# Loading the first weight of a two-layer recurrence: which queues carry its four chunks, and which engine clears two small tiles

## The chip, the cores and the metric

The kernel runs on one core of a Trainium2 chip. A core has a matrix engine (TensorE, PE in the profile), three engines for elementwise work (VectorE or DVE, ScalarE or ACT, GpSimd or POOL) and a synchronisation engine (SyncE or SP). Loads and stores are done by 16 DMA engines that the core's queues share; a transfer is *issued* by an instruction on SyncE, ScalarE or GpSimd and *lands* some microseconds later, when its completion semaphore is counted up. The metric is the device time of one execution in microseconds. The kernel before takes 1639.33 us, the median of three runs from 1638.49 to 1639.35.

## What is computed

The input x has 128 sequences of 128 steps with 512 features, all in fp32. Two recurrent layers follow one another, each added to its input:

```python
# layer 0, for each step t; Wh, Wz are the two halves of W
gate = sigmoid(h @ Wh.T + z_t @ Wz.T + b)
h    = tanh(h * (1 - alpha) + gate * z_t)      # z = x, h starts as cond
x    = x + hs
# layer 1, for each step t
h    = tanh(x_t @ Wx + b + h @ Wh)             # h starts as cond
x    = x + hs
```

The products of the input with Wz and with Wx don't depend on the state and can be done for several steps at once; the products of the state with the two Wh are done step by step.

## The kernel before, in words

The features lie on the 128 partitions in 4 blocks, the sequences on the free axis, so that one step of x is a tile of 128 x 512. Tiles arrive in the natural order and VectorE transposes them in blocks of 32 x 32 (lines 198 to 216). Steps go in groups of four. Layer 1 follows layer 0 by nine steps. The input products of a group are done with a fast scheme of seven products in place of eight, for most groups nested in itself; those of the first steps are done plainly (`input_product`, line 467, its matmuls at L475), and the first nested group (steps 4 to 7) plainly with one level (L357). `state_product` (L464) does a step's state products.

The order of work is written by hand: `at(time, fn, ...)` enters a call into a plan, the plan is sorted by the time given, and every call then records its instructions in that order, so each engine's own instruction order follows from the plan. The times are only sorting keys; what runs when is settled by semaphores.

Around the change, at the start, the plan does the following:

- `clear_small` (line 166) writes zeros to `condT` (128 x 512, later the transposed start state) and to `rows` (32 x 96, into which three small vectors are loaded later, L172). `warm_up` (line 181) does five matmuls on the zeros of `condT`, into banks that are not read.
- `load_x` (line 125) loads a step of x in four quarters of 32 partitions, 64 KB each, going round the queues that it is given (L128). `both` is SyncE and ScalarE.
- `load_w0(1, "wz", chunks, engines)` (line 138) loads Wz in four chunks m = 0 to 3; a chunk is again four quarters of 64 KB, going round the queues given (L147). Without queues it goes to SyncE and ScalarE in turn.
- As the chunks come, `transpose_w0` (L212, VectorE) turns one chunk after the other, and `input_product` multiplies step 0 with it on TensorE; then step 1, then the plain products of group 1 (L357), for which steps 4 to 7 are transposed by VectorE and added up (L238) by VectorE and GpSimd.
- `load_w0(0, "wh0")` loads the state weight of layer 0, `load_cond` the start state; the state products begin after the plain products of group 1.

Transfers don't each have a semaphore of their own. The transfers of SyncE and ScalarE together go round eight completion semaphores (lanes), four for each as they alternate here, and those of GpSimd round another eight. An issue that comes back to a lane first waits until the lane's previous transfer has landed. So SyncE's fifth issue waits for its first to land, and GpSimd's ninth for its first.

Within the first 13 us the issues before are, in order: SyncE and ScalarE each x0 (2), chunk 0 (2), chunk 2 (2), chunk 3 (2), x5 (2), x7 (2), then the state weight (2) and cond (2); GpSimd chunk 1 (4), x1 (4), x4 (4), x6 (4), small rows (3). The x7 issues also wait until the tile of x0 is free again (five x tiles are there).

The functions that the change touches, with the line numbers of the profile:

Of the kernel before, what the change touches and what calls it, by code (L numbers as in the profile page):

```python
# [13 lines left out]
def kernel(  # L14
# [35 lines left out]
    nc = tc.nc  # L50
# [23 lines left out]
    def at(time, fn, *args):  # L74
        plan.append((time, len(plan), fn, args))
# [47 lines left out]
    both = (nc.sync, nc.scalar)  # L123
# [35 lines left out]
    rows = const.tile([S, 3, S], F32, tag="rows", name="rows")  # L159
# [4 lines left out]
    condT = const.tile([P, C, P], F32, tag="condT", name="condT")  # L164

    def clear_small():
        nc.gpsimd.memset(condT, 0.0)
        nc.gpsimd.memset(rows, 0.0)

    def load_small():  # L170
        for i, v in enumerate((b0, alpha, b1)):
# [377 lines left out]


    at(0.0, clear_small)
    at(0.01, warm_up)
    at(0.1, load_x, 0, both)
    at(0.2, load_w0, 1, "wz", (0,))
    at(0.21, load_w0, 1, "wz", (1,), (nc.gpsimd,))
    at(0.22, load_w0, 1, "wz", (2, 3))
    at(0.3, load_x, 1, (nc.gpsimd,))
    at(0.31, load_x, 4, (nc.gpsimd,))
    at(0.4, load_x, 5, both)
    at(0.41, load_x, 6, (nc.gpsimd,))  # L560
# [166 lines left out]
```

## Time and profile before

| what | before |
|---|---|
| median of 3 runs | 1639.33 us |
| the profiled execution's own time | 1639.27 us |
| its span, first to last instruction | 1637.4 us |
| first GpSimd issue (chunk 1) | 1.40 us |
| x0 transposed from | 4.70 us |
| chunks 0, 1, 2, 3 transposed from | 6.64, 7.65, 8.75, 10.81 us |
| first product with Wz from | 7.41 us |
| product with chunk 3 from | 11.58 us |
| first state product from | 26.51 us |

The page gives the busy time of each engine and its share of the span. A chain of waits is followed back from the last instruction: at each step to what released it. The timeline lists instructions by start, duration, engine, line, operation and tiles, with the idle time before and what ended it in brackets; a "q" behind the engine's name marks its instruction queue, which issues transfers. L147 is line 147 of the kernel. Times inside the execution count from the span's start.

### The profile page before, as it was taken

What the parts mean: (1) busy time and instruction counts of PE and PEld (TensorE: products, weight loads), DVE (VectorE), ACT (ScalarE), POOL (GpSimd) and SP (SyncE); (2) the same over time, 40 slices, a digit from 0 to 9 for tenths busy, and PEclk for the clock granted to TensorE, in tenths of its full rate; (3) what the DMA queues carried; (4) which work ended last, traced back from release to release, by engine and by line L of the source; (5) the groups of instructions that cost most, each with busy time, mean ns of one, the idle gap of its engine ahead of it and who ended that gap; (6) DMA issues with size and microseconds to landing.
All of it is one profiled execution on the core that took longest, in us unless ns stands there. A gap on an engine that the chain in (4) does not pass through costs nothing.

```text
span 1637.4 us, 36984 instructions
## 1 busy us (share of the span) xinstructions
PE 1628.1 (99%) x14420; PEld 1621.8 (99%) x14420; DVE 1315.5 (80%) x2958; ACT 791.4 (48%) x2047; POOL 666.6 (41%) x548
## 2 busy tenths in 40 slices
PE   9999999999999999999999999999999999999998
PEld 8999999999999999999999999999999999999998
DVE  6677888878888888888787888888878888878785
ACT  2545445544454444444554545445545454454454
POOL 5553433344334333443344334433443344334442
PEclk9999999999999999999999999999999999999999
DMA  8201221121112111221112111211111112111113
GB/s 176 53 18 40 46 46 40 40 47 46 40 40 48 45 40 40 46 47 40 40 45 48 40 40 44 49 40 40 45 43 45 39 42 51 40 40 29 26 21 65
DMA packets 152078, 73.99 MB, mean 45 GB/s; under 512 B 16992, under 2 KB 150624, under 8 KB 151904
## 3 DMA queue, kind: packets, MB, share of 16 engines
q1 hardware_dynamic: 147936, 69.01, 18.7%
q10 hardware_dynamic: 3360, 1.57, 0.5%
q8 instruction: 113, 1.85, 0.5%
q0 software_dynamic: 608, 1.06, 0.3%
q14 instruction: 61, 0.50, 0.1%
HBM read 38.02 MB, written 33.55 MB: 44 GB/s over the span
## 4 chain that ended last, share of the span: by engine, by line
PE 96%; DVE 1%; ACT 1%; issue 1%; DMA 1%; POOL 0%; ACTq 0%; SPq 0%; DVEq 0%; POOLq 0%
PE r0a L464 14%; PE r0b L464 14%; PE r1b L464 14%; PE r1a L464 13%; PE B_b L363 12%; PE A_a L363 11%; PE A_b L363 9%; PE B_a L363 8%; DMA wz_in<-in_L_cond_W_dram 1%; PE A_a L357 0%; PE r1a L475 0%; DVE h L512 0%; PE B_a L357 0%; PE r0a L475 0%; PE B_b L357 0%
## 5 line engine op out<-in xcount | busy, mean ns | idle before, releaser
L520 POOL TENSOR_TENSOR T<-T,h 128x512 f32<-128x512 f32 x255 | 325.4, 1276 | 947.5 <-ACT h L517 880.8
L464 PE MATMUL r0a<-h,wha 128*128 128x128 f32 x2032 | 248.0, 275 | 0.2
L464 PE MATMUL r0b<-h,whb 128*128 128x128 f32 x2032 | 247.9, 275 | 0.0
L464 PE MATMUL r1a<-h,wha 128*128 128x128 f32 x2032 | 247.6, 275 | 0.0
L464 PE MATMUL r1b<-h,whb 128*128 128x128 f32 x2024 | 246.8, 275 | 0.0
L517 ACT ACTIVATE h<-h 128x256 f32<-128x256 f32 x256 | 106.7, 417 | 280.2 <-DVE h L512 278.7
L464 PEld LDWEIGHTS r0a<-h,wha 128*128 128x128 f32 x2032 | 237.4, 192 | 0.9 <-DVE r0a L452 0.5
L464 PEld LDWEIGHTS r0b<-h,whb 128*128 128x128 f32 x2032 | 237.1, 192 | 0.1
L464 PEld LDWEIGHTS r1a<-h,wha 128*128 128x128 f32 x2032 | 237.1, 192 | 0.0
L464 PEld LDWEIGHTS r1b<-h,whb 128*128 128x128 f32 x2024 | 236.2, 192 | 0.0
L503 ACT ACTIVATE r0a<-r0a,per_feature 128x128 f32<-128x128 f32 x256 | 87.6, 342 | 104.2 <-PE r0a L464 100.1
L509 DVE TENSOR_TENSOR r0a<-r0a,T 128x256 f32<-128x256 f32 x128 | 55.0, 429 | 84.1 <-ACT r0a L503 84.1
L509 DVE TENSOR_TENSOR r1a<-r1a,T 128x256 f32<-128x256 f32 x128 | 55.3, 432 | 67.7 <-ACT r1a L503 67.7
L205 DVE STREAM_TRANSPOSE o<-T 128x512 f32<-128x512 f32 x127 | 89.5, 705 | 4.1 <-POOL T L520 3.6
L200 DVE STREAM_TRANSPOSE T<-x 128x512 f32<-128x512 f32 x128 | 86.9, 682 | 6.0 <-DMA x<-in_x_dram 5.0
L503 ACT ACTIVATE r1a<-r1a,per_feature 128x128 f32<-128x128 f32 x256 | 85.2, 333 | 4.2
L530 ACT ACTIVATE h<-r1b,per_feature 128x128 f32<-128x128 f32 x255 | 80.4, 370 | 7.7 <-PE r1b L464 5.4
L530 ACT ACTIVATE h<-r0b,per_feature 128x128 f32<-128x128 f32 x256 | 78.0, 355 | 11.1 <-PE r0b L464 9.3
L238 POOL TENSOR_TENSOR S_b<-T 128x512 f32<-128x512 f32 x64 | 82.0, 1281 | 0.2
L512 DVE SCALAR_TENSOR_TENSOR h<-h,leak,r0a 128x128 f32<-128x128 f32 x254 | 77.0, 345 | 5.2
L512 DVE SCALAR_TENSOR_TENSOR h<-h,leak,r1a 128x128 f32<-128x128 f32 x254 | 77.0, 345 | 4.5
L391 ACT COPY ca<-A_a 128x896 f32<-128x896 f32 (+1 forms) x31 | 27.7, 895 | 101.7 <-PE A_a L363 101.7
(221 smaller groups left out, 3723.9 us busy)
## 6 DMA issues: line engine op xcount, KB each, us to landing
out_dram<-o SPq DMA_DIRECT2D x510, 64.0 KB, 1.8
x<-in_x_dram SPq DMA_DIRECT2D x494, 64.0 KB, 2.3
wx_in<-in_L_cond_Wx_dram SPq DMA_DIRECT2D x4, 256.0 KB, 5.4
wh_in<-in_L_cond_Wh_dram SPq DMA_DIRECT2D x4, 256.0 KB, 8.7
x<-in_x_dram POOLq DMA_DIRECT2D x12, 64.0 KB, 4.2
wh_in<-in_L_cond_W_dram SPq DMA_DIRECT2D x2, 256.0 KB, 6.3
wh_in<-in_L_cond_W_dram ACTq DMA_DIRECT2D x2, 256.0 KB, 6.8
x<-in_x_dram ACTq DMA_DIRECT2D x6, 64.0 KB, 4.2
```

The costliest lines, as they stand in the source:

```text
L200: nc.vector.transpose(dst.rearrange("p c (a i) -> p c a i", i=S), src.rearrange("p a (c j) -> p c a j", j=S))
L205: nc.vector.transpose(dst.rearrange("p a (c j) -> p c a j", j=S), src.rearrange("p c (a i) -> p c a i", i=S))
L238: eng.tensor_tensor(out(which), one(), two(), op)
L363: nc.tensor.matmul(sets[tag][:, n], self.right(outer, i), self.left(g, outer, i), start=first and n % 4 == 0, stop=True, skip_group_check= ...
L391: nc.scalar.copy(self.part(g, 1, 0)[:, n], sets[tag][:, n])
L464: nc.tensor.matmul(banks[m * (len(banks) - 1)][0][:, m], self.wh[:, c, 2 * half + m, :], h[t - 1][:, c], start=alone and n == 0, stop=c == ...
L503: nc.scalar.activation(gate[:, m], gate[:, m], AF.Sigmoid, bias=per_feature[:, 0, f : f + 1])
L509: nc.vector.tensor_tensor(gate, gate, at_of(t)[:, two[i]], ALU.mult)
L512: nc.vector.scalar_tensor_tensor(h0[t][:, f], h0[t - 1][:, f], leak[:, f : f + 1], gate[:, m], ALU.mult, ALU.add)
L517: nc.scalar.activation(h0[t][:, two[i]], h0[t][:, two[i]], AF.Tanh)
L520: (eng or nc.gpsimd).tensor_tensor(at_of(t)[:, part], at_of(t)[:, part], h[t][:, part], ALU.add)
L530: nc.scalar.activation(h1[t][:, f], ps[:, m], AF.Tanh, bias=per_feature[:, 2, f : f + 1])
```

## The change

The two clears are recorded on VectorE in place of GpSimd. Chunk 0's four quarters go to GpSimd, GpSimd, SyncE and ScalarE. Chunk 1 goes to SyncE and ScalarE, chunks 2 and 3 to GpSimd. The load of x1 goes from GpSimd to SyncE and ScalarE, behind the chunks in the plan as before. Nothing else changes in what is loaded or computed.

```diff
     def clear_small():
-        nc.gpsimd.memset(condT, 0.0)
-        nc.gpsimd.memset(rows, 0.0)
+        nc.vector.memset(condT, 0.0)
+        nc.vector.memset(rows, 0.0)
...
     at(0.0, clear_small)
     at(0.01, warm_up)
     at(0.1, load_x, 0, both)
-    at(0.2, load_w0, 1, "wz", (0,))
-    at(0.21, load_w0, 1, "wz", (1,), (nc.gpsimd,))
-    at(0.22, load_w0, 1, "wz", (2, 3))
-    at(0.3, load_x, 1, (nc.gpsimd,))
+    at(0.2, load_w0, 1, "wz", (0,), (nc.gpsimd, nc.gpsimd, nc.sync, nc.scalar))
+    at(0.21, load_w0, 1, "wz", (1,))
+    at(0.22, load_w0, 1, "wz", (2,), (nc.gpsimd,))
+    at(0.23, load_w0, 1, "wz", (3,), (nc.gpsimd,))
+    at(0.3, load_x, 1, both)
     at(0.31, load_x, 4, (nc.gpsimd,))
     at(0.4, load_x, 5, both)
     at(0.41, load_x, 6, (nc.gpsimd,))
```

The issues are then, in order: SyncE and ScalarE each x0 (2), chunk 0 (1), chunk 1 (2), x1 (2), x5 (2), x7 (2), state weight (2), cond (2); GpSimd chunk 0 (2), chunk 2 (4), chunk 3 (4), x4 (4), x6 (4), small rows (3). On VectorE the two clears stand ahead of the transpose of x0.

## The prediction

> **What bounds the kernel now.** I read the page first, then the waits of TensorE, then the chain of the first 14 us, then the timeline and single transfers there. The page's span and busy lines:
>
> ```profile
> span 1637.4 us, 36984 instructions
> PE 1628.1 (99%) x14420; PEld 1621.8 (99%) x14420; DVE 1315.5 (80%) x2958; ACT 791.4 (48%) x2047; POOL 666.6 (41%) x548
> ```
>
> TensorE is busy for all but 9.3 us of the span, and the table by stage has it at 500.00 of 500.00 us between 500 and 1000. So what this change can give lies in the few idle microseconds of the start, and it reaches the end one for one. The waits of TensorE, us in total, times, longest:
>
> ```profile
> PE r0a L475 <- DVE wa L212: 1.4, 1, 1.4
> PE r0b_-1_99 L185 <- POOL condT L167: 1.3, 1, 1.3
> PE r1a L475 <- DVE wa L212: 0.9, 1, 0.9
> PE B_b L363 <- DVE cb L387: 0.6, 1, 0.6
> ```
>
> Two waits on the transposed first weight (1.4 and 0.9 us) are all that the change aims at; the 1.3 us is the start of the warm-up. The chain of waits of the first 14 us (start, duration, what):
>
> ```profile
> 2.19 4.26 DMA wz_in<-in_L_cond_W_dram
> ...
> 6.47 4.15 DMA wz_in<-in_L_cond_W_dram
> ...
> 10.81 0.72 DVE wa L212
> ...
> 11.58 1.16 PE r1a L475 x8
> 12.74 1.34 PE r0a L475 x12
> ```
>
> Two transfers stand one behind the other: ScalarE's fourth issue (chunk 0, at 2.19) lands at 6.45, and only then may ScalarE issue its eighth (the last quarter of chunk 3, at 6.47), because each queue reuses a completion lane after four issues. It lands at 10.62, VectorE transposes from 10.81, TensorE starts on it at 11.58 and then has no gap: 27.40 us busy of the 27.40 from 11.60 to 39.00. The moment 11.58 is what the change must move. From the timeline, GpSimd and VectorE:
>
> ```profile
> 0.75 0.52 POOL L167 MEMSET condT<- 128x512 f32 x1 [0.29 <-POOLq L713]
> 1.21 0.17 POOL L168 MEMSET rows<- 32x96 f32 x1
> 1.40 2.35 POOL L147 DMA_DIRECT2D wz_in<-in_L_cond_W_dram  x4
> ...
> 6.64 0.71 DVE L212 STREAM_TRANSPOSE wa<-wz_in 128x512 f32<-128x512 f32 x1 [1.23 <-DMA wz_in<-in_L_cond_W_dram]
> ...
> 7.65 0.71 DVE L212 STREAM_TRANSPOSE wa<-wz_in 128x512 f32<-128x512 f32 x1 [0.29 <-DMA wz_in<-in_L_cond_W_dram]
> ```
>
> GpSimd loses 0.65 us to clearing before its first issue, and VectorE's transposes of chunks 0 and 1 each wait for a landing. Last, the stage table (PE, PEld, DVE, ACT, POOL busy, clock, DMA share, GB/s), and then GpSimd's issues of x (ns min/median/max):
>
> ```profile
> 7.40:10.70 3.30, 3.27 (x24) 2.90 (x24) 1.42 (x2) 0.00 (x0) 3.12 (x7) 1.00 1.14 236
> ```
>
> ```profile
> L128 POOL DMA_DIRECT2D x<-in_x_dram x12: 548/548/551, 3.7 to 10.0; - x12
> ```
>
> The DMA engines are full (share 1.14) at 236 GB/s, so 64 KB takes 0.28 us of them. One GpSimd issue takes 0.55 us (the first of all 0.71).
>
> **The change part by part.** *The two clears* go from GpSimd to VectorE, which does nothing until 4.70. No row shows VectorE clearing; GpSimd's clear took 0.52 us, and VectorE's passes over 128x512 take 0.65 to 0.71. So condT is ready at 1.27 to 1.46 and the warm-up starts between 0.06 us earlier and 0.13 later than its 1.33. I take zero: x0 hides it (lands at 4.50), and the warm-up ends before the first product. GpSimd's first issue moves from 1.40 to 0.75.
>
> *Chunk 0.* GpSimd issues its first two quarters at 0.75 and 1.46, SyncE and ScalarE one each as their third issues (1.66 and 1.70). GpSimd's second transfer of before landed 4.2 us after its issue: 1.46 + 4.2 = 5.66. ScalarE's third landed at 5.39; with one more transfer ahead, 5.67. So chunk 0 is complete near 5.7 instead of 6.45, its transpose starts at 5.9 (0.19 later, as before) and TensorE at 6.66 (0.77 after the transpose's start, as before) instead of 7.41.
>
> *Chunk 1* leaves GpSimd for SyncE and ScalarE, as their fourth and fifth issues. The fifth waits for the queue's first x0 transfer. ScalarE's fifth of before was issued at 3.30 and landed 4.5 us later, at 7.82. GpSimd now has five transfers issued by 3.3 instead of four, 0.28 each, and x0 itself may be late by as much: 7.8 to 8.4. Transpose at 8.0 to 8.6, product at 8.8 to 9.35. TensorE did three chunks from 7.41 to 10.68, 1.09 each, so chunk 2 is done at 11.0 to 11.5. Chunk 1 gets later by 0.2 to 0.8 us against 7.52, GpSimd's landing of before.
>
> *Chunks 2 and 3* go to GpSimd as its issues 3 to 10. Issue 6 is at 3.66, so chunk 2 lands by 3.66 + 4.2 = 7.9, before 8.56 of now. Issue 10 is at 0.75 + 0.71 + 8 x 0.55 = 5.86. Its lane is that of GpSimd's second issue (eight lanes there), landed at 5.66, so there is no wait. GpSimd's issues at 5.36 and 5.90 landed 4.3 and 4.1 later: chunk 3 is in at 9.95 to 10.15 instead of 10.62, and could be multiplied from 10.9 to 11.1.
>
> *The later loads.* SyncE and ScalarE each issue one transfer fewer before x5, x7, the state weight and cond, all of which come one slot sooner. x1 goes to them as sixth and seventh issues, gated by landings at about 4.2 to 5.7, so in by 9.9; VectorE transposes it only after chunk 3, near 11.0 instead of 11.45. On GpSimd x4, x6 and the three small rows stand two issues later, less 0.65: 1.10 - 0.65 = 0.45 us. x4 lands near 12.3 (before: 11.94), and VectorE, which took it at 12.61, takes it near 12.4. x6 lands near 14.9 (14.45); VectorE took it at 14.57, then x7 at 15.56 after a wait of 0.28 for its landing. x7 now comes first, so both are done by 16.4 instead of 16.27. The sums over them follow at 16.31 and end at 17.72; TensorE first wants them at 19.39, so the slack is 1.67 us, less what the start gains. The rows, now gated by VectorE's clear too, land near 17.4 (16.87) and are read at 23.83. The state weight lands sooner than 20.63; first read at 20.82 and needed at 26.30. All of this costs nothing while those margins stand; x6 landing 1.2 us later than reckoned would start to cost.
>
> *The sum.* Chunk 3 is multiplied from the later of 10.9 to 11.1 (its own landing) and 11.0 to 11.5 (end of chunk 2). I take 11.1, as chunk 1's landing has its nearest row at the early end (the fifth ScalarE issue, whose gate is unchanged). 11.58 - 11.1 = 0.5 us earlier, and nothing behind has a gap. Ends for the unknowns: -0.7 and +2.1 (below). The profiled execution of before took 1639.27, 1.87 outside its span; 0.5 less is 1638.8. The median shown is 1639.33, 0.06 above; from there it is also 1638.8.
>
> **Two rules of the Trainium skill against this.** The rows first: transfers landed nearly in the order of issue whichever queue issued them (4.50 for x0's last, 10.62 for chunk 3's last), with the engines full. "DMA: Bandwidth & Descriptors", section "Issuing engines are not separate DMA queues", says that starting transfers from several engines saves only the issuing time. By it alone the gain is the one transfer that GpSimd starts earlier, 0.28 us, and the time 1639.0; my sum adds what the lane waits give. The second: GpSimd's issues took 548 to 551 ns though VectorE's transposes at 4.70, 6.64 and 8.75 ran beside them. "SBUF — State Buffer", section "SBUF: two separate sides", says that certain VectorE operations lock GpSimd out of writing descriptors; were the clears such, GpSimd would start at 1.40 as before, chunk 3 would come at 10.65 and the time would be 1639.3. No trace here shows a VectorE clear.
>
> **The rivals.** *A, hidden by chunk 1:* the fifth issues on SyncE and ScalarE land late (8.4 or later), TensorE does chunks 1 to 3 back to back from 9.4, chunk 3 starts at 11.5. For it: full engines, two GpSimd transfers ahead. Against: the gate, x0's landing, hardly moves. Time 1639.3.
>
> *B, slower, GpSimd's queue as the bound:* ten weight transfers now go through one queue that keeps only its share of full engines. SyncE's and ScalarE's shares let four transfers through each from chunk 0's end (6.45) to chunk 3's (10.62), 1.04 us apiece. Ten at that pace from the first packet (2.3: the trace has its first packets 1.6 us after the issue at 1.40, now at 0.75) end at 12.7, 2.1 us later than 10.62: 1641.4. Against: until 12 us GpSimd's queue moved 0.95 of 2.38 MB, 40% and not a third; at that rate its ten would take 6.3 us. It decides once a GpSimd transfer takes over 0.83 us, (10.62 - 2.3) / 10.
>
> *C, the clock:* the warm-up's ten passes are 0.43 us apart, the same shape in L357 is 1.73 / 8 = 0.22 apart, and L475 runs fast from 7.41, so the clock rose between. With warm-up or first product moved, the rise may come after chunk 0; each chunk at half speed costs about 0.9 us, of which only what falls after 10.9 counts: 0 to 2 us, 1640.3 in the middle. Against: the warm-up moves by 0.13 at most.
>
> **How the numbers follow.** Forecast (0.3 to 0.7 us faster) 0.61, A 0.19, B 0.12, C or another disturbance of the start 0.08. A measurement of this kernel tells 0.2%, 3.3 us, from no change; nearly all of these lie inside. Faster than that would need more than the 2.3 us of waiting there is: 0.03. Slower than that needs B and C together or a cause that I don't see: 0.07. The rest, 0.90, is the same. The forecast's own range is 1638.3 to 1639.1, with the 0.9 us by which the shown runs differ; the full range, 1637.9 to 1640.6, takes A, the spread below and the nearer half of B and C.
>
> **What would show it.** In the changed trace: GpSimd's first issue at 0.75 and its tenth at 5.9; transposes of chunks at about 5.9, 8.2, 8.9 and 10.2; the product of chunk 3 at 11.1 and no gap after; the sums over x6 and x7 done by 18; waits of TensorE on L212 of some 0.7 us and under 0.5 us at chunks 0 and 3. Wrong would be: a GpSimd issue over 0.6 us, a landing over 5 us after its issue, first products 0.2 us apart, or TensorE waiting on L238.

## The result and the profile after

The changed kernel takes 1642.58 us (median of 13 runs, 1642.21 to 1644.27), the kernel before 1639.35 us (13 runs, 1638.49 to 1640.10). The ratio is 1.0021, with a 95% interval of 1.0014 to 1.0028: 3.2 us slower, where 0.5 us faster was forecast. Of the 3.2 us, 2.8 lie in the span (1640.3 in the median, against 1639.35 - 1.87 = 1637.5) and 0.4 outside it (2.3 us against 1.87, nearly the same in every run of a kernel). The profiled execution, 1643.36 us, is 0.8 us above the median. One execution of the changed kernel in its repeat at the end of the experiments, the only one of that repeat with a profile, ran at a granted clock of 0.85 and took 1840.39 us; it is left out of every number below.

The page of the changed kernel, its span and its busy time:

```profile
span 1641.0 us, 36981 instructions
PE 1630.2 (99%) x14420; PEld 1623.5 (99%) x14420; DVE 1316.2 (80%) x2960; ACT 791.5 (48%) x2047; POOL 667.4 (41%) x548
```

The waits of TensorE in the changed kernel (us in total, times, longest):

```profile
PE A_a L357 <- DVE S_a L238: 2.0, 1, 2.0
PE r0b_-1_99 L185 <- DVE condT L167: 1.5, 1, 1.5
PE B_a L357 <- DVE ca L387: 0.8, 1, 0.8
PE B_b L363 <- DVE cb L387: 0.6, 1, 0.6
PE r0a L475 <- DVE wa L212: 0.5, 1, 0.5
PE r1a L475 <- DVE wa L212: 0.2, 1, 0.2
```

The two waits on the transposed weight did shrink, from 1.4 and 0.9 us to 0.5 and 0.2, but nothing ended sooner by it: the 1.6 us that they lost went into the first 16 passes on TensorE, which took 3.78 us where they took 2.16 before. Two waits are new: 2.0 us for the sums over x6 and x7 (L238) and 0.8 us for VectorE's addition behind them (L387). The timeline of VectorE and TensorE in the changed kernel shows where they come from (start, duration, engine, line, operation, tiles; in brackets the idle time before):

```profile
6.62 3.78 PE L475 MATMUL r0a<-T,wa 128*128 128x128 f32 x16 [0.53 <-DVE wa L212]
...
10.98 0.71 DVE L212 STREAM_TRANSPOSE wa<-wz_in 128x512 f32<-128x512 f32 x1 [1.79 <-DMA wz_in<-in_L_cond_W_dram]
...
11.75 1.16 PE L475 MATMUL r1a<-T,wa 128*128 128x128 f32 x8 [0.24 <-DVE wa L212]
...
19.03 1.30 DVE L200 STREAM_TRANSPOSE T<-x 128x512 f32<-128x512 f32 x2 [3.33 <-issue]
20.37 0.69 DVE L238 TENSOR_TENSOR S_a<-T 128x512 f32<-128x512 f32 x1
...
21.93 1.97 PE L357 MATMUL A_a<-S_a,wca 128*128 128x256 f32 x8 [2.00 <-DVE S_a L238]
...
24.72 1.99 PE L357 MATMUL B_a<-S_a,wca 128*128 128x256 f32 x8 [0.82 <-DVE ca L387]
```

Chunk 3 is transposed from 10.98 (before: 10.81) and multiplied from 11.75 (11.58): the path that was to get 0.5 us shorter is 0.17 longer. Then VectorE stands still for 3.33 us and transposes x6 and x7 from 19.03; before, x6 was at 14.57. The profile writes "issue" there, since no event in it ended the wait, but the next view names the transfer. It is the chain of waits of the changed kernel (start, duration, what):

```profile
5.83 4.66 DMA wz_in<-in_L_cond_W_dram
10.49 0.28 issue
10.78 6.86 DMA x<-in_x_dram
17.64 1.40 issue
19.03 0.06 DVE T L200
```

GpSimd's ninth issue (chunk 3) goes out at 5.83 and lands at 10.49. That frees the lane for its seventeenth, the third quarter of x6, at 10.78. The eighteenth follows at 11.32 and lands at 18.95, 7.6 us later; before, x6's last quarter was issued at 9.96 and landed 4.5 us later. So of the 4.5 us by which x6 is late, 1.4 are the later issue and 3.1 the longer way. GpSimd's timeline, and the time from issue to landing of x6's last quarter by itself (us, min/median/max):

```profile
1.33 5.59 POOL L147 DMA_DIRECT2D wz_in<-in_L_cond_W_dram  x10 [0.89 <-POOLq L714]
6.92 1.09 POOL L128 DMA_DIRECT2D x<-in_x_dram  x2
8.19 2.27 POOL L128 DMA_DIRECT2D x<-in_x_dram  x4 [0.18 <-issue]
10.78 1.09 POOL L128 DMA_DIRECT2D x<-in_x_dram  x2 [0.33 <-DMA wz_in<-in_L_cond_W_dram]
```

```profile
DMA to landing us min/median/max: 7.6/7.6/7.6
```

What stands in between is the state weight, four transfers of 256 KB. Its issues, and GpSimd's last issues of x (the last of the five is at 9.96), in the kernel before:

```profile
7.80 2.70 POOL L128 DMA_DIRECT2D x<-in_x_dram  x5 [0.17 <-issue]
11.07 1.52 SPq L147 DMA_DIRECT2D wh_in<-in_L_cond_W_dram  x2
11.89 1.42 ACTq L147 DMA_DIRECT2D wh_in<-in_L_cond_W_dram  x2
```

The issues of the state weight in the changed kernel:

```profile
10.45 1.35 SPq L147 DMA_DIRECT2D wh_in<-in_L_cond_W_dram  x2
10.68 1.40 ACTq L147 DMA_DIRECT2D wh_in<-in_L_cond_W_dram  x2
```

Before, all of x6 was issued (by 9.96) ahead of the first of them (11.07). Now SyncE and ScalarE have one transfer fewer each in front and issue the first two at 10.45 and 10.68, while GpSimd has two more in front: the first half of the state weight is ahead of half of x6.

### The profile page after: what moved, and what is told of

Read it like the earlier page. It is cut to its first block, busy times and chain, and to the rows that moved or that the text cites. A ratio compares the mean times of both kernels' runs of the same rounds, so it can differ in the third digit from the quotient of the medians.

```text
span 1641.0 us, 36981 instructions
## 1 busy us (share of the span) xinstructions
PE 1630.2 (99%) x14420; PEld 1623.5 (99%) x14420; DVE 1316.2 (80%) x2960; ACT 791.5 (48%) x2047; POOL 667.4 (41%) x548
## 4 chain that ended last, share of the span: by engine, by line
PE 95%; DVE 1%; issue 1%; DMA 1%; ACT 1%; POOL 0%; SPq 0%; DVEq 0%; ACTq 0%; POOLq 0%
PE r0a L464 14%; PE r0b L464 14%; PE r1b L464 14%; PE r1a L464 13%; PE B_b L363 12%; PE A_a L363 11%; PE A_b L363 9%; PE B_a L363 8%; DMA x<-in_x_dram 0%; DVE h L512 0%; DMA wz_in<-in_L_cond_W_dram 0%; POOL wz_in L147 0%; PE r1a L475 0%; PE B_a L357 0%; PE A_a L357 0%
## 5 line engine op out<-in xcount | busy, mean ns | idle before, releaser
L238 POOL TENSOR_TENSOR S_b<-T 128x512 f32<-128x512 f32 x64 | 82.0, 1281 | 0.2
L238 POOL TENSOR_TENSOR S_a<-T 128x512 f32<-128x512 f32 x60 | 76.8, 1280 | 0.2 <-DVE T L200 0.2
```

The lines of the kernel that those rows point to most:

```text
L238: eng.tensor_tensor(out(which), one(), two(), op)
```

## The experiments

*Theory T*: the loss in the span is x6 behind the state weight. *Rival U*: the clears on VectorE are the loss. *Rival V*: chunk 3's own landing, or the half-speed first products, are.

**One part alone.** The clears on VectorE in the kernel before:

```diff
-        nc.gpsimd.memset(condT, 0.0)
-        nc.gpsimd.memset(rows, 0.0)
+        nc.vector.memset(condT, 0.0)
+        nc.vector.memset(rows, 0.0)
```

> The kernel before with the two clears on VectorE and nothing else. Theory T (the 3.2 us are x6 landing late, at 18.95 instead of 14.45, because its last two issues on GpSimd now stand behind the state weight's 256 KB transfers): the clears alone leave x6 in place, the sums over x6 and x7 (L238) start near 16.3 and the time is 1639.3, within 0.6 us. Rival U (the clears are the loss: a slower GpSimd start, a later clock, or time outside the span, which rose from 1.87 to 2.3 us): at least half of the loss, 1640.9 or more.

1639.56 us against 1639.41, ratio 1.0001 (0.9992 to 1.0010): nothing. The sums start at 16.26. U falls for the time as a whole, though the time outside the span is 2.14 us here against 1.88 for the kernel before. The other part alone is the changed kernel with these four lines turned back:

> The changed kernel with the two clears back on GpSimd. Theory T: x6 lands past 17 us, TensorE waits 1.5 to 2.5 us on the sums (L238) and the time is 1641.5 to 1643. Rival U (the clears are the loss): 1640.5 or less.

1644.57 us, ratio 1.0032 (1.0019 to 1.0044), beyond the upper end that was given. The sums wait 2.8 us for x6, whose last quarter was issued at 11.51 and landed at 20.07. So the queues alone make the loss, and a larger one; that the clears on VectorE should save 2 us beside them was not expected, and is taken up at the end of this section.

**x6 taken from behind the state weight, by queue.**

```diff
-    at(0.41, load_x, 6, (nc.gpsimd,))
+    at(0.41, load_x, 6, both)
```

> The changed kernel with the load of x6 on SyncE and ScalarE, behind x5 and ahead of x7 and the state weight. Theory T: x6 lands by 14.5, TensorE has no wait on L238, and 2.8 of the 3.2 us come back: 1639.3 to 1640.2. Rival V (it is chunk 3, landing at 10.90 instead of 10.62, or the half-speed first products): chunk 3's product still starts near 11.75 and the time stays at 1642 or more.

1640.00 us against 1639.41, ratio 1.0003 (0.9994 to 1.0011). 2.6 of the 3.2 us are back: 2.1 in the span (its excess over the kernel before falls from 2.8 to 0.7 us) and 0.5 outside it, for which x6 is no explanation. TensorE's waits in this kernel:

```profile
PE r0a L475 <- DVE wa L212: 1.5, 2, 0.9
PE r0b_-1_99 L185 <- DVE condT L167: 1.5, 1, 1.5
PE r1a L475 <- DVE wa L212: 1.3, 1, 1.3
PE B_b L363 <- DVE cb L387: 0.6, 1, 0.6
```

L238 and the L387 wait behind it are gone. Chunk 3's product starts at 11.86, no earlier than in the changed kernel, so V's cause is still there. It costs 0.28 us up to the first state product (26.79 against 26.51); where the other 0.4 us of the span's excess arise isn't shown.

**x6 ahead of the state weight by order alone.** The same queues, but cond's four 64 KB transfers issued before the state weight:

```diff
-    at(4.0, load_cond)
+    at(3.75, load_cond)
```

> The changed kernel with the four 64 KB transfers of cond issued ahead of the state weight's four of 256 KB, nothing moved between queues. If the bytes of the state weight ahead of x6 are the cause: x6's last two issues stay near 10.8 and 11.3, the state weight's first near 12.5, so x6 lands by 16.5, no wait on the sums (L238), 1639.8 to 1640.6. If the late issue by itself decides: 1642 or more.

1640.60 us against 1639.23, ratio 1.0008 (0.9999 to 1.0017). x6's last issue is at 11.47, even a little later than in the changed kernel, and lands in 5.2 us instead of 7.6:

```profile
DMA to landing us min/median/max: 5.2/5.2/5.2
```

So the late issue alone is not it; most of the loss hangs on what is ahead of it in the DMA engines. A wait of 0.5 us on L387 stays, and of the 1.4 us that are left 0.4 lie outside the span.

**The size of what is ahead.** The state weight in sixteen transfers of 64 KB:

```diff
-    at(3.8, load_w0, 0, "wh0")
+    at(3.8, load_w0, 0, "wh0", (0, 1, 2, 3))
```

> The changed kernel with the state weight loaded in sixteen transfers of 64 KB in place of four of 256 KB, on the same queues. If what holds x6 back is the bytes of the state weight that stand ahead of it in the DMA engines, x6's last transfers land 4.5 to 5.5 us after their issue instead of 6.9 and 7.6, the sums start near 17 to 18 and the time is 1640 to 1641. If it is the wait of GpSimd's issues for their lanes (issued at 10.78 and 11.32 instead of 9.42 and 9.96) that decides, the latency doesn't matter and the time stays within 0.5 us of 1642.6.

x6's last quarter, issued at 11.33, lands in 5.0 us, and the sums start at 17.76, as expected. But the time is 1641.95 us (ratio 1.0015, 1.0006 to 1.0024), not 1640 to 1641. A new wait took the place of the old one; TensorE's longest wait and ScalarE's timeline show it:

```profile
PE A_a L357 <- ACT ka_p L374: 1.6, 1, 1.6
```

```profile
10.72 7.90 ACTq L147 DMA_DIRECT2D wh_in<-in_L_cond_W_dram  x8
18.73 0.97 ACTq L179 DMA_DIRECT2D cond_in<-in_cond_dram  x2
19.74 1.28 ACT L374 ACT_TABLE_LOAD   x1 [19.74 <-DMA wh_in<-in_L_cond_W_dram]
21.03 0.59 ACT L374 COPY ka_p<-A_a 128x512 f32<-128x512 f32 x1
```

ScalarE issues its ten transfers one lane wait after the other until 19.70, and its first copy out of PSUM (18.08 before) stands behind them at 21.03. The expectation had counted only the transfers, not what queues behind their issues. So this run shows what sets x6's landing, but not what the landing costs.

**Is a late x6 enough?** The kernel before, with only the three small rows issued ahead of x6:

```diff
-    at(0.41, load_x, 6, (nc.gpsimd,))
-    at(0.42, load_small)
+    at(0.41, load_small)
+    at(0.42, load_x, 6, (nc.gpsimd,))
```

> The kernel before with the three small rows issued ahead of x6 on GpSimd, so that x6's last issues come near 11 to 11.5, beside the state weight's first. Theory T says that x6's landing alone makes the loss: TensorE's wait on L238 is the landing + 2.85 - 19.4 us (two transposes 1.30, two sums 1.45, 0.1 of start), nothing below 16.55, and the time rises by 1.0 to 1.4 of it; with a landing between 16 and 18.5 the time is 1639.4 to 1642. If x6 lands past 17 and the time stays at 1639.4, theory T is wrong.

1641.43 us against 1639.23, ratio 1.0013 (1.0004 to 1.0022). x6's last quarter is issued at 12.29 and lands at 18.11, and the changed kernel's two waits appear in the kernel before:

```profile
PE r0a L475 <- DVE wa L212: 2.1, 1, 2.1
PE r0b_-1_99 L185 <- POOL condT L167: 1.3, 1, 1.3
PE A_a L357 <- DVE S_a L238: 1.0, 1, 1.0
PE B_a L357 <- DVE ca L387: 0.8, 1, 0.8
```

The formula gives 18.11 + 2.85 - 19.4 = 1.56 us, and the wait is 1.0, as step 0's products ended 0.4 us later in that execution too. The median rose by 2.2 us, inside the range given. But the landing of 18.11 belongs to the profiled execution, whose span is 2.8 us longer, 1.8 times 1.56 and more than the 1.0 to 1.4 expected, since the L387 wait comes on top.

**GpSimd's first issue.** It came at 1.33, not at 0.75. In this kernel the clears and the warm-up stand behind the transpose of x0; `rows` is thereby cleared after its loads, so the small vectors are zero and VectorE waits long for them, and only the first issue is read from it:

```diff
-    at(0.0, clear_small)
-    at(0.01, warm_up)
+    at(3.65, clear_small)
+    at(3.66, warm_up)
```

> The changed kernel with the two clears and the warm-up recorded behind the transpose of x0, so that VectorE does nothing beside GpSimd's first issue. If the clears on VectorE hold GpSimd back, its first issue comes at 0.75 instead of 1.33; if GpSimd's start has another cause, it stays at 1.33. The warm-up starts near 5 us, so the first products may run at half speed; the time is not the question.

GpSimd and VectorE in it:

```profile
1.31 5.59 POOL L147 DMA_DIRECT2D wz_in<-in_L_cond_W_dram  x10 [0.86 <-POOLq L714]
```

```profile
4.21 0.71 DVE L200 STREAM_TRANSPOSE T<-x 128x512 f32<-128x512 f32 x1 [4.21 <-DMA x<-in_x_dram]
4.98 0.48 DVE L167 MEMSET condT<- 128x512 f32 x1
```

With VectorE idle until 4.21, GpSimd still issues first at 1.31. So the clears on VectorE don't hold it back, and the clears that GpSimd did before (0.75 to 1.38) fitted into this start almost whole. What the start consists of no view shows.

**A version that might beat both.** Every queue issues as many transfers as before, but chunk 3 goes ahead of half of x1 (with the clears on VectorE):

```diff
-    at(0.22, load_w0, 1, "wz", (2, 3))
-    at(0.3, load_x, 1, (nc.gpsimd,))
+    at(0.22, load_w0, 1, "wz", (2,))
+    at(0.23, load_w0, 1, "wz", (3,), (nc.gpsimd, nc.gpsimd, nc.sync, nc.scalar))
+    at(0.3, load_x, 1, (nc.gpsimd, nc.gpsimd, nc.sync, nc.scalar))
```

> The kernel before with the clears on VectorE, and with chunk 3 and x1 each split over GpSimd, GpSimd, SyncE and ScalarE, so that every queue issues as many transfers as before and x6 keeps its place. Chunk 3's issues move ahead of half of x1: GpSimd's at 3.7 and 4.2, the others as seventh... fifth of chunk 3 at 4.8 to 5.5, all landed by 9.5 instead of 10.3 to 10.6, TensorE multiplies chunk 3 near 10.4, and the time is 1638.2 to 1638.9. If the landing order doesn't follow the issue order, or another load is late for it: 1639.4 or more.

1639.52 us against 1639.23, ratio 1.0002 (0.9993 to 1.0011): no gain. Chunk 3 is in at 9.94, not by 9.5, and the wait for it is gone from TensorE's list, but another is there:

```profile
PE r0b_-1_99 L185 <- DVE condT L167: 1.5, 1, 1.5
PE r0a L475 <- DVE wa L212: 1.4, 1, 1.4
PE B_b L363 <- DVE cb L387: 0.6, 1, 0.6
PE r0a L475 <- DVE h L512: 0.5, 1, 0.5
```

VectorE waits 1.20 us for the last of SyncE's early loads of x (landed at 35.9; in the kernel before, the same stretch of five transposes has no wait) and the state comes late, at 39.3. The first state product began at 26.24 against 26.51: of the 0.7 us won at chunk 3 (10.90 against 11.58), 0.4 was gone by then and the rest was given back at 39.3, where the kernel before waits 0.13 and this one 0.47.

**The clears beside the new queues.** The changed kernel and the one with its clears on GpSimd, again, on one chip:

> The changed kernel once more, beside the next one. If the queues and the clears act together, as the runs so far say, it stays near 1642.6, x6's last issue near 11.3 lands near 19, and the wait on L238 is about 2.0 us.

> The changed kernel with the clears on GpSimd, once more, on the same chip as the one above. If GpSimd's 0.07 us later start is carried on by its lane waits (its tenth issue waits for its second to land), x6's last issue is 0.2 us later than above, behind one more of the state weight's transfers, lands about 1 us later, and the time is 1 to 2 us above. If the 2 us between the two was a difference of chips, they now agree within 0.5 us.

1643.50 us (ratio 1.0025, 1.0016 to 1.0035) and 1644.23 us (1.0028, 1.0018 to 1.0039). Together they spread over 1641.9 to 1645.1. The 2 us between the two has shrunk to 0.7, with overlapping intervals, which is neither of the two outcomes that were named: the explanation by GpSimd's start is not confirmed, and whether the clears matter here stays open. The landing and the wait expected of the changed kernel weren't measured. What the repeat does show is that the landing of x6 varies within one kernel. In the profiled execution of queues_again x6's last quarter was issued at 11.31 and landed at 17.79; in that of queues_only it was issued at 11.51 and landed at 20.07, and the spans were 1639.9 and 1642.2. What made the difference isn't shown. It was issued before SyncE's second state weight transfer in both (11.53 and 11.54), with a lead of 0.22 and 0.03 us, but a lead of 0.21 in late_clears (11.12 and 11.33) went with 7.7 us to landing, not with the 6.5 of queues_again.

Put together, the profiled executions whose x6 lands late give one line (late_clears is left out, as VectorE waits there for other loads). B_a is TensorE's second product with the sums, the one that waits on L387:

| kernel | x6's last quarter landed | B_a from | B_a after the landing | span | span less the landing |
|---|---|---|---|---|---|
| cond_first | 16.63 | 22.40 | 5.77 | 1637.9 | 1621.3 |
| queues_again | 17.79 | 23.55 | 5.76 | 1639.9 | 1622.1 |
| x6_late_before | 18.11 | 23.99 | 5.88 | 1640.2 | 1622.1 |
| changed | 18.95 | 24.72 | 5.77 | 1641.0 | 1622.1 |
| queues_only | 20.07 | 25.84 | 5.77 | 1642.2 | 1622.1 |
| before, for comparison | 14.45 | 21.33 | 6.88 | 1637.4 | - |

(queues_only and queues_again are the same kernel in two executions.) In the four that land past 17 us every microsecond of x6's landing is one of the span, whatever else was changed. The path that sets it is VectorE's: two transposes, two sums, two additions of weights (L248), then L387. cond_first is on the same line at B_a. Its span is 0.8 us below; a wait of 0.6 us that all the others have (B_b on L387, far behind the start) is absent from its list, which is most of that.

## Why the prediction was wrong

*What bounds the kernel* held: TensorE is full and the start carries over one for one. The first state product came at 30.0 instead of 26.51, 3.5 us later, and the span of that execution is 3.6 longer.

*"x6 lands near 14.9 (14.45)" failed, and it made most of the loss.* It took GpSimd's eighteenth issue at 0.45 us after that of before and its latency as unchanged, 4.5 us. Measured: it was issued at 11.32, 1.36 us later than before, and took 7.6 us to landing, as the state weight's transfers now stood ahead. Of the 0.91 us by which the issue missed the forecast, 0.58 are GpSimd's later start (below), and 0.33 are the wait of the seventeenth issue, just ahead of it, for the ninth to land (10.49). The same paragraph noted that the state weight comes "one slot sooner" and counted that as harmless; it was costed by its own need and not by what it passes.

*The margin behind x6 was too wide as well.* x6 was said to cost from 1.2 us beyond 14.9, that is 16.1, because the sums (L238) have that slack. The tighter path is the L387 addition behind them, which the forecast left out: B_a comes 5.77 us after the landing and was at 21.33 before, so x6 starts to cost from about 15.6 (an estimate, 21.33 - 5.77). With chunk 3's product 0.5 us earlier, as forecast, it would have been 15.1, a margin of 0.2 us. The landing at 18.95 is beyond all three.

*"GpSimd's first issue moves from 1.40 to 0.75" failed.* It moved to 1.33. The work taken off GpSimd had been hidden in a start that it has anyway. Those 0.58 us are more than the whole forecast gain: the tenth issue went out at 6.38 instead of 5.86 and landed at 10.90 instead of 10.15. Chunk 3's product came at 11.75 here, and at 11.6 to 12.1 in the other kernels with these queues. The forecast gain was therefore never there; x6_hw, which has everything but x6's lateness, is at 1640.0.

*"Transpose at 8.0 to 8.6" for chunk 1 was too late.* It came at 7.44 here and at 7.47 to 8.14 in the other kernels with these queues. *Right:* GpSimd's issues of 0.55 us each. *Right by luck:* chunk 0 was transposed at 5.86 (5.9) and multiplied from 6.62 (6.66), but GpSimd's second transfer went out 0.58 us later than forecast (2.04) and landed 3.7 us later instead of 4.2; and the waits on L212 came to 0.7 us as forecast, because the first products were slow and not because chunk 3 was early. *The signs of being wrong:* three of the four occurred, a landing over 5 us after its issue (7.6), first products 0.2 us apart (3.78 / 16 = 0.24) and the wait on L238.

*The rivals.* A (hidden) describes what the queues are worth with x6 out of the way, but not for its reason: chunk 3's landing set the end, not chunk 1's. B (GpSimd's queue as the bound) had the right queue and the wrong load: its ten weight transfers landed 3.1 to 4.7 us after their issue, near the rows of before, and it was x6 behind them that came late. C's slow first products occurred and cost nothing here: the first 16 passes took 3.78 us where they took 2.16 before, and chunk 2 was still done at 11.51, 0.24 ahead of chunk 3's product. That the clock was the reason isn't shown: the profile's granted clock reads 1.00 from 6.60 to 10.20. Nor does it need the change: in x6_late_before, with the warm-up of the kernel before, the same passes took 3.44 us. *The two rules:* what the Trainium skill, "DMA: Bandwidth & Descriptors", section "Issuing engines are not separate DMA queues", says of spreading transfers (only issuing time is saved) is not contradicted by x6_hw, which has no gain over the kernel before once x6 is in time (1640.00 against 1639.41). The lock of GpSimd by VectorE ("SBUF — State Buffer", section "SBUF: two separate sides") did not appear with these clears: first issue at 1.31 without a clear beside it, 1.33 with one. Issues of 0.71, 0.56 and 0.55 us are the same in both.

*Chances:* 3.2 us is 0.2%, on the edge between same and slower; slower had 0.07, and what happened is the "cause that I don't see" of that sentence. The measured time lies 2.0 us above the full range.

## What to carry to other kernels

When a load is moved between queues, list for every queue what moves *up* as well as what moves down, and look for the large transfer that passes a small one which somebody waits for: a 64 KB transfer issued just after two of 256 KB took 7.6 us instead of 4.5. With eight completion lanes in rotation, as GpSimd has them here, a slip of one issue can come back eight issues later (the seventeenth waited 0.33 us for the ninth). A margin is to be taken at every consumer behind the late load, not only at the first: here the second one was the tighter. And work taken off an engine at the start is worth something only if the engine would otherwise have been able to begin.

## What was not expected of the hardware

- GpSimd's first transfer is issued at 1.31 to 1.33 us even with only four small constants before it (done by 0.45), 0.57 us after those of SyncE and ScalarE (0.74), and its first issue takes 0.71 us, the others 0.55 or 0.56.
- Execution times spread more in the two kernels with x6 and the state weight side by side, 1641.9 to 1645.1 us, than in the kernel before on the same chip, 1638.9 to 1639.9; x6's landing differs from one execution to the next (17.79 and 20.07), but that this is the whole of the spread isn't shown.
- The time outside the span differs from kernel to kernel and hardly within one: 1.9 us for the kernel before, 2.3 for the changed one, 2.1 for clears_only, 1.8 for x6_hw. It is 0.4 of the 3.2 us, and its cause was not found.
